# A decoder's block turn through DRAM: one VectorE transpose for 512 columns, 8 KB tiles, 2 KB stores, loads of two chunks, and later small loads at the start

## The chip, the cores and the metric

One core of a Trainium2 chip runs the whole kernel as one launch. The metric is the device time in microseconds of that launch. The kernel before took 2060.33 us, the median of three executions (2054.5 to 2066.38).

## The reference, cut to what matters

Two decoder layers act on x of shape (4, 512, 512) in float32. Each layer has three residual steps, and each step starts with a layer norm of x:

```python
x = x + attn0(layernorm(x))     # 16 query heads of 32, one key/value head        stage L0
x = x + xattn0(layernorm(x))    # mixes columns with a softmax made from ctx_1024  stage X0
x = x + ffn0(layernorm(x))      # 4-bit weights, 1408 inner, rms norm              stage FF
x = x + attn1(layernorm(x))     # 16 heads of 32                                   stage L1
x = x + xattn1(layernorm(x))    # 16 heads of 128, 8 key/value heads, ctx_1024     stage X1
x = x + ffn1(layernorm(x))      # 32 experts of rank 16, top 2                     stage R1
```

Stage X1 is the longest. For each of 4 batches and 16 heads it computes softmax(q k^T / sqrt(128)) as a 512 x 512 matrix and multiplies it by v. The softmax is made with tokens on the partitions. The product with v needs it turned, with keys on the partitions.

## The kernel before, in words

A batch's 512 tokens are QT = 4 tiles of 128 tokens, and its 512 columns are KC = 4 chunks of 128. x stays in SBUF as 16 tiles of 128 x 512 float32. To keep float32 accuracy on TensorE, an operand is split into a high and a low part (`split_sbuf`, L704: a cast to fp32r, on ScalarE or VectorE, and then a subtraction, on GpSimd or VectorE). `three` (L649) makes three matmuls for every product: high by high, high by low, low by high.

**Order of the work.** The kernel does not issue its instructions as it is written. `put` and `after` (L615, L621) place pieces of work on a time axis. Run in that order, they are recorded as tasks, and `arrange` (L327) plays a list scheduler on them with a cost for each instruction: each engine takes the ready task of the highest priority, and a tile is given a slot when a slot of its pool is free. Priorities come from a pass backwards from the end. 16 rounds are played, and the shortest plan gives the order on each engine and the slot of each tile. The times in `put` fix only the first round's order; no task waits for its `put` time. All tasks are then issued at L1845, the only line that the profile shows for them. Each engine works its queue strictly in order, SyncE's DMA queue (SP) too.

**Pools.** Per partition there are TBUFS = 50 tiles "t" of 2 KB (activations, high and low parts, the `ws` and `pt` landing tiles) and WBUFS = 17 tiles "w" of 4 KB (split weights, attention stacks, FF weights, and `tr`).

**The block turn** (`block_turn`, L756) turns four tiles of 128 tokens x 512 columns into four chunks of 128 columns x 512 tokens. It is used 79 times: for the 64 heads of X1 (tiles `pe`) and for 15 of the layer norms in FF, L1, X1 and R1 (tiles `h`). It has three steps:

- `turn(t)`: VectorE transposes tile t in blocks of 32 x 32, as two instructions of 256 columns into two `tr` tiles of the "w" pool, 8 instructions a turn.
- `away(j)`: for each half j, four stores on SP write `tr` to a DRAM scratch `turn`, 128 KB each, in pieces of 512 bytes. That is 8 stores a turn.
- `back(k)`: for each chunk k, one load on SP brings 256 KB, 2 KB a partition, into a "t" tile `pt`. Then `split_sbuf` makes `turnedh` and `turnedl`, which TensorE reads. That is 4 loads a turn.

In X1 a head's scores, `turn`, `away`, `back` and product with v (`weigh`) are placed about one period PER_X1 = 11.7 us apart in the plan (L1650 to L1657).

**The start.** x of batch 0 is loaded by SP (L573). `cols`, `mask8` and `scales16` are loaded on ScalarE's queue (L576 to L580). VectorE then makes `desc`, `scales` and `maskf` (L599 to L604) ahead of the first layer norm. `scales` is used from FF on, `maskf` from X1 on, `desc` in R1. The x of batches 1 to 3 are loaded by three 1 MB transfers, placed at -11, -10 and -9 us (L1034).

Of the kernel before, what the change touches and what calls it, by code (L numbers as in the profile page):

```python
# [10 lines left out]
F32 = mybir.dt.float32  # L11
# [22 lines left out]
NI = FI // P  # L34
# [3 lines left out]
LN_EPS = 1e-5  # L38
RMS_EPS = 1e-6
BIG = 1e30  # L40
TBUFS = 50
WBUFS = 17
START = 45.0
DQ = 50.0
PER_L0, PER_X0, PER_F1, PER_L1, PER_X1, PER_R1 = 16.5, 12.5, 6.1, 22.5, 11.7, 25.0
# [16 lines left out]
WARM = 24  # L62
LOOK = {"tensor": 99999, "vector": 99999, "scalar": 99999, "gpsimd": 99999, "sync": 99999}
T_X0, PER_A0 = 5.0, 15.0
NA = {"L0": 4, "X0": 4, "FF": 0, "L1": 0, "X1": 0, "R1": 0}
EARLY = "v1", "qk1", "o1"
ACT_JIT = True
EVAC = "AA01"
DT = 6
# [9 lines left out]
TINY = 2.0**-14  # L79
# [469 lines left out]
def decoder_kernel(ctx: ExitStack, tc: tile.TileContext, a: dict, out: bass.AP):  # L549
# [8 lines left out]
    nc = Recorder()  # L558
    PSUM = bass.MemoryType.PSUM

    def pool(name, bufs, n=None, **k):
        return Pool_(ctx.enter_context(tc.tile_pool(name=name, bufs=bufs or 1, **k)), bufs, n or name)

    base = pool("base", None)
    small = pool("small", 4)
    wp = pool("weights", WBUFS)
    tp_ = pool("tiles", TBUFS)
    dram = pool("scratch", None, space=bass.MemoryType.DRAM)
    ps = pool("ps", 1, space=PSUM)

# [4 lines left out]
    cols = base.tile([P, 19], F32, name="cols")  # L575
    nc.scalar.dma_start(cols, a["cols"])  # L576
    mask8 = base.tile([P, NB * QT], U8, name="mask8")
    nc.scalar.dma_start(mask8, a["mask_col"])
    scales16 = base.tile([P, 2 * NI * KC + NI * NT], F16, name="scales16")
    nc.scalar.dma_start(scales16, a["gu_cols"])  # L580
    scales = base.tile([P, 2 * NI * KC + NI * NT], F32, name="scales")
    ident = base.tile([P, P], F32, name="ident")
    make_identity(real, ident.real())
# [12 lines left out]
    desc_i = base.tile([P, NS], I32, name="desc_i")  # L596
    nc.gpsimd.iota(desc_i, pattern=[[-1, NS]], base=NS, channel_multiplier=0)
    desc = base.tile([P, NS], F32, name="desc")
    nc.vector.tensor_copy(desc, desc_i)  # L599
    n = 2 * NI * KC  # L600
    nc.vector.tensor_scalar(scales[:, 0:n], scales16[:, 0:n], 1.0 / TINY, None, ALU.mult)
    nc.vector.tensor_copy(scales[:, n:], scales16[:, n:])
    maskf = base.tile([P, NB * QT], F32, name="maskf")
    nc.vector.tensor_copy(maskf, mask8)  # L604


    warm = ps.pool.tile([P, S], F32, name="warm", tag="mm.0", bufs=1)
# [48 lines left out]
    def at(pr, *ix):  # L656
        return pr[0][ix], pr[1][ix]
# [72 lines left out]
    def weight(t, key, src, cols=None, keep=False):  # L730


        got = {}

        def load():
            if key in stored:
                got["w"] = wp.tile(stored[key].tile.shape, F32R, tag="w", name="w")
                nc.sync.dma_start(f32(got["w"]), f32(stored[key]))
            else:
                got["w"] = split_weight(key, src, cols, keep, act=ACT_JIT and keep)  # L740

# [14 lines left out]
    def block_turn(tiles, got):  # L756


        tr, dr = [None] * 2, [None] * 2

        def turn(t):
            for j in range(2):
                if t == 0:
                    tr[j] = wp.tile([P, 2 * S], F32, tag="w", name="tr")
                nc.vector.transpose(
                    tr[j].rearrange("p (b t i) -> p b t i", t=QT, i=HD)[:, :, t, :],
                    tiles[t][:, j * 2 * P : (j + 1) * 2 * P].rearrange("p (b i) -> p b i", i=HD),
                )

        def away(j):  # L770
            dr[j] = dram.tile([2, P, HG, P], F32, tag="turn", name="turn", bufs=DT)
            for n in range(HG):
                nc.sync.dma_start(
                    dr[j][:, :, n, :].rearrange("c (q j) n -> j (c q) n", j=HD),
                    tr[j][n * HD : (n + 1) * HD, :].rearrange("j (b n) -> j b n", n=P),
                    run=4 * P,
                )

        def back(k):
            pt = T(name="pt")  # L780
            nc.sync.dma_start(pt, dr[k // 2][k % 2].rearrange("p a n -> p (a n)"))
            got[k] = pair(name="turned")
            split_sbuf(
                [g.rearrange("p (t a i) -> p a t i", t=QT, a=HG) for g in got[k]],
                pt.rearrange("p (a t i) -> p a t i", t=QT, a=HG),
                3.5,
                True,
            )

        return (  # L790
            [lambda t=t: turn(t) for t in range(QT)],
            [lambda j=j: away(j) for j in range(2)],
            [lambda k=k: back(k) for k in range(KC)],
        )

# [112 lines left out]
    def group(t0, per, u, keys, values, done, on_dve, lead):  # L908
# [122 lines left out]
        e = t0 + per + SUMS  # L1031
        put(e, e, [sums])

    for b in range(1, NB):  # L1034
        put(
            -12 + b,
            -12 + b,
            [
                lambda b=b: nc.sync.dma_start(
                    x[:, b * QT : (b + 1) * QT, :], a["x"][b].rearrange("(t p) d -> p t d", p=P)  # L1040
                )
            ],
        )
# [56 lines left out]
    for b in range(NB):  # L1100
        tb = now + 4 * b * per - (A0 + 0.25) * per
        hT = layernorm_T(tb - (0.25 + LN0) * per, tb - 0.25 * per, b, NA["L0"], pool=b < SL)
        kv = {}
# [24 lines left out]
        for c in range(KC):  # L1128
            t0 = now + (4 * b + c) * per
            u = {}  # L1130

            def queries(pq, u=u, c=c):
# [7 lines left out]
                lambda k, c=c: wq0[k](slice(c * P, (c + 1) * P)),  # L1140
# [106 lines left out]
    for b in range(NB):  # L1247
# [148 lines left out]
    for i in range(NI):  # L1396
        t = DQ + (ff0 + NI * per - 45 - DQ) * i / NI
# [12 lines left out]
    for b in range(NB):  # L1410
        tb = now + 4 * b * per - (A1 + 0.2) * per
        hT = layernorm_T(tb - LN1 * per, tb, b, NA["L1"], b in DV["L1"])

# [20 lines left out]
        for k in range(QT):  # L1434
# [5 lines left out]
                lambda c, k=k, hT=hT, wv=wv: (at(hT[c], ALL, tok(k)), wv[c]()),  # L1440
                lambda pv, k=k, f=values: f(pv, k),
            )
        oT = []
        for c in range(KC):
            t0 = now + (4 * b + c) * per
            u = {}
            for j in range(2):
                n0 = j * D + c * P
                w = weight(
                    t0 - (A1 + 0.5 - 0.2 * j) * per,  # L1450
                    ("qk1", j, c),
                    chunks(a["wqkv1"][:, n0 : n0 + P]),
                    KC,
                    keep=True,
                )

                def turned(pq, j=j, c=c, u=u):
# [13 lines left out]
                    lambda k, w=w: w(slice(k * P, (k + 1) * P)),  # L1471
# [5 lines left out]
            def normalise(w, pd, c=c, oT=oT):  # L1477
# [18 lines left out]
                lambda h, k, v=v, c=c: v[k][:, (4 * c + h) * HD : (4 * c + h + 1) * HD],  # L1496
# [10 lines left out]
        for t in range(QT):  # L1507
# [5 lines left out]
                lambda c, t=t, oT=oT, wo=wo: (at(oT[c], ALL, tok(t)), wo[c]()),  # L1513
                lambda po, t=t, b=b: add_to_x(b * QT + t, po),
# [6 lines left out]
    for b in range(NB):  # L1521
        tb = now + NH * b * per
        cT = context(tb - 3.2 * per, b)
        hT = layernorm_T(tb - 1.9 * per, tb - 1.1 * per, b, NA["X1"], b in DV["X1"])
        mk = {}
# [8 lines left out]
        for g in range(4):  # L1534
# [21 lines left out]
            for j in range(2):  # L1556
# [28 lines left out]
            for i in range(4):  # L1585
# [9 lines left out]
                u = {"pe": [None] * QT, "pT": [None] * QT}  # L1595

                def queries(pq, u=u):
# [6 lines left out]
                    lambda k, w=wq: w(slice(k * P, (k + 1) * P)),  # L1604
# [326 lines left out]
```

## Time and profile before

| what | value |
|---|---|
| three executions | 2054.5, 2060.33, 2066.38 us |
| the profiled execution's own time | 2058.85 us |
| its span, first to last instruction | 2057.1 us |
| DVE / ACT / POOL busy | 90% / 60% / 58% of the span |
| DMA, q1 (SP's queue) | 349472 packets, 465.50 MB, 72.7% of 16 engines |
| chain that ended last | PE 65%, DVE 12%, DMA 12% |

The profile is read by stage. L0 ends near 340 us, X0 near 405, FF near 720, L1 near 1150, X1 near 1950, and R1 runs to the end. The profile's waits name what ended an engine's idle time. A row of instruction groups gives the busy time, the mean nanoseconds of one, and the idle time before them. All work has the line L1845, so rows are told apart by tile names.

### The profile page before, as it was taken

To read this page: it belongs to the slowest core of one execution; us is meant where nothing else is said; L and a number is where in the kernel's file an instruction comes from. 1 tells how busy PE (TensorE), PEld (TensorE's weight loads), DVE (VectorE), ACT (ScalarE), POOL (GpSimd) and SP (SyncE) were. 2 spreads that over 40 slices of the span, in tenths; PEclk is the share of its full clock that TensorE was granted. 3 is DMA by queue.
4 is the path that set the end of the run, shared out by engine and by line. 5 is a ranking of instruction groups with operands and counts; after the bars stand their busy time and mean duration, and the time that the engine had idled before them with its cause. 6 is when DMAs were issued, how large, how long until landed. Compare 5 with 4: busy or idle time off the path is not lost.

```text
span 2057.1 us, 31942 instructions
## 1 busy us (share of the span) xinstructions
PE 1984.3 (96%) x9728; PEld 1476.8 (72%) x9728; DVE 1848.7 (90%) x3645; ACT 1239.2 (60%) x2461; POOL 1195.0 (58%) x930
## 2 busy tenths in 40 slices
PE   7999999999999999999999999999999999999999
PEld 6755554778877856565656777787888777887677
DVE  8999998999999889898899898999999889998883
ACT  5876767467757355454546767676666557555520
POOL 5688889378777466867577445454454244233610
PEclk9999999999999999999999999999999999999999
DMA  7554444656758777777764889999999899988911
GB/s 254 198 187 149 144 159 145 232 185 231 261 171 296 222 229 240 211 243 221 222 169 141 246 236 272 288 288 294 299 299 304 246 307 292 317 255 247 273 60 58
DMA packets 350075, 467.57 MB, mean 227 GB/s; under 512 B 28944, under 2 KB 211472, under 8 KB 349904
## 3 DMA queue, kind: packets, MB, share of 16 engines
q1 hardware_dynamic: 349472, 465.50, 72.7%
q8 instruction: 77, 1.26, 0.3%
q14 instruction: 94, 0.77, 0.1%
q10 hardware_dynamic: 432, 0.04, 0.0%
HBM read 291.36 MB, written 173.93 MB: 226 GB/s over the span
## 4 chain that ended last, share of the span: by engine, by line
PE 65%; DVE 12%; DMA 12%; ACT 5%; issue 2%; SPq 2%; POOL 1%; ACTq 0%; DVEq 0%; POOLq 0%
PE mm L1845 65%; DMA pt<-turn 6%; DVE pe L1845 2%; SPq L1845 2%; DVE tr L1845 2%; DMA stack<-stack 2%; DVE nm L1845 2%; DMA turn<-tr 2%; ACT pT L1845 1%; DMA stack<-ql 1%; DVE x L1845 1%; ACT turnedh L1845 1%; ACT pe L1845 1%; DVE ol L1845 1%; DVE ql L1845 1%
## 5 line engine op out<-in xcount | busy, mean ns | idle before, releaser
L1845 POOL TENSOR_TENSOR turnedl<-pt,turnedh 128x512 fp32r<-128x512 f32 x249 | 328.8, 1334 | 407.2 <-ACT turnedh L1845 181.7
L1845 PE MATMUL mm<-turnedh,w 128*128 128x512 f32 x1120 | 414.6, 398 | 7.8 <-ACT turnedh L1845 3.0
L1845 DVE TENSOR_REDUCE nm<-mm 128x1 f32<-128x512 f32 x512 | 323.3, 678 | 35.3 <-PE mm L1845 34.5
L1845 PE MATMUL mm<-stack 96*128 96x512 f32 (+1 forms) x1024 | 325.8, 422 | 25.6 <-DMA stack<-stack 17.7
L1845 ACT ACTIVATE pT<-mm 128x512 f32<-128x512 f32 x512 | 273.2, 609 | 78.9 <-PE mm L1845 70.4
L1845 POOL TENSOR_TENSOR acc<-acc,pT 128x512 f32<-128x512 f32 x200 | 271.0, 1378 | 31.5 <-DVE acc L1845 12.6
L1845 PEld LDWEIGHTS mm<-stack 96*128 96x128 f32 (+1 forms) x1024 | 186.1, 192 | 140.5 <-issue 35.4
L1845 PE MATMUL mm<-turnedl,w 128*128 128x512 f32 x736 | 282.8, 394 | 1.2 <-POOL turnedl L1845 1.2
L1845 PEld LDWEIGHTS mm<-turnedh,w 128*128 128x128 f32 x1120 | 211.2, 189 | 65.7 <-ACT gu L1845 7.8
L1845 ACT ACTIVATE pe<-pe,nmc 128x512 f32<-128x512 f32 x256 | 184.6, 722 | 112.6 <-DVE nmc L1845 105.9
L1845 ACT CAST turnedh<-pt 128x512 fp32r<-128x512 f32 x291 | 176.5, 617 | 113.5 <-DMA pt<-turn 105.7
L1845 PE MATMUL mm<-w,oh 128*128 128x512 f32 x640 | 203.9, 391 | 5.6 <-ACT oh L1845 5.6
L1845 POOL TENSOR_TENSOR acc<-pT 128x512 f32<-128x512 f32 x118 | 155.6, 1333 | 77.2 <-ACT pT L1845 60.9
L1845 DVE STREAM_TRANSPOSE tr<-pe 128x256 f32<-128x256 f32 x512 | 198.3, 419 | 2.2 <-ACT pe L1845 2.0
L1845 DVE CUSTOM_DVE_ANT_0 pe<-mm,mb 128x512 f32<-128x512 f32 x256 | 169.7, 670 | 4.9 <-PE mm L1845 4.3
L1845 POOL TENSOR_TENSOR w<-ws,w 128x512 fp32r<-128x512 f32 x93 | 126.0, 1364 | 70.1 <-ACT w L1845 41.2
L1845 PEld LDWEIGHTS mm<-turnedl,w 128*128 128x128 f32 x736 | 139.1, 189 | 26.5 <-POOL turnedl L1845 2.7
L1845 ACT ACTIVATE gu<-mm,scales 128x512 f32<-128x512 f32 x173 | 113.5, 691 | 57.5 <-PE mm L1845 56.8
L1845 PEld LDWEIGHTS mm<-w,oh 128*128 128x128 f32 x640 | 118.9, 188 | 32.1 <-ACT oh L1845 8.0
L1845 POOL TENSOR_TENSOR gu<-gu 128x512 f32<-128x512 f32 x83 | 109.7, 1333 | 44.4 <-DVE gu L1845 33.0
L1845 DVE SCALAR_TENSOR_TENSOR gu<-mm,scales,gu 128x512 f32<-128x512 f32 x176 | 122.1, 738 | 2.4 <-PE mm L1845 2.3
L1845 PE MATMUL mm<-w,ol 128*128 128x512 f32 x320 | 123.7, 391 | 0.0
(235 smaller groups left out, 4543.9 us busy)
## 6 DMA issues: line engine op xcount, KB each, us to landing
turn<-tr SPq DMA_DIRECT2D x632, 128.0 KB
pt<-turn SPq DMA_DIRECT2D x316, 256.0 KB
w<-scr SPq DMA_DIRECT2D x148, 512.0 KB
stack<-stack SPq DMA_DIRECT2D x96, 384.0 KB
scr<-w SPq DMA_DIRECT2D x56, 512.0 KB
stack<-qh SPq DMA_DIRECT2D x96, 256.0 KB
w<-gu SPq DMA_DIRECT2D x44, 512.0 KB
w<-dn SPq DMA_DIRECT2D x44, 384.0 KB
```

Of the source, the lines that this page charges most:

```text
L1845: got = getattr(getattr(real, t.engine), name)(*[made(v) for v in a_], **{n: made(v) for n, v in k.items()})
```

## The change

The transpose of a tile becomes one instruction of 512 columns into one 8 KB tile `tr` of a new pool "big" with 2 slots. Four stores of 256 KB in 2 KB pieces replace eight of 128 KB in 512-byte pieces. Two loads of 512 KB in 1 KB pieces, into a 4 KB "w" tile `pt` that holds two chunks, replace four of 256 KB in 2 KB pieces. The pool "t" goes from 50 to 44 tiles and "w" from 17 to 16. `mask8` and `scales16` are loaded on SP and placed at 40 us, their four VectorE casts 4 us later; the x of batches 1, 2 and 3 are placed at -5, 50 and 110 us.

```diff
-TBUFS = 50
-WBUFS = 17
+TBUFS = 44
+WBUFS = 16
+BBUFS = 2
...
+T_X = -5.0, 50.0, 110.0
+T_TABLES = 40.0
...
-    nc.scalar.dma_start(mask8, a["mask_col"])
...
-    nc.scalar.dma_start(scales16, a["gu_cols"])
...
-    nc.vector.tensor_copy(desc, desc_i)
-    n = 2 * NI * KC
-    nc.vector.tensor_scalar(scales[:, 0:n], scales16[:, 0:n], 1.0 / TINY, None, ALU.mult)
-    nc.vector.tensor_copy(scales[:, n:], scales16[:, n:])
...
-    nc.vector.tensor_copy(maskf, mask8)
...
         def turn(t):
-            for j in range(2):
-                if t == 0:
-                    tr[j] = wp.tile([P, 2 * S], F32, tag="w", name="tr")
-                nc.vector.transpose(
-                    tr[j].rearrange("p (b t i) -> p b t i", t=QT, i=HD)[:, :, t, :],
-                    tiles[t][:, j * 2 * P : (j + 1) * 2 * P].rearrange("p (b i) -> p b i", i=HD),
+            if t == 0:
+                u["tr"] = big.tile([P, KC * S], F32, tag="b", name="tr")
+
+            nc.vector.transpose(
+                u["tr"].rearrange("p (e c t i) -> p c e t i", e=HG, c=KC, t=QT)[:, :, :, t, :],
+                tiles[t].rearrange("p (c e i) -> p c e i", c=KC, e=HG),
+            )
+
+        def away(n):
+            if n == 0:
+                u["dr"] = dram.tile([P, HG, KC * P], F32, tag="turn", name="turn", bufs=DT)
+            nc.sync.dma_start(
+                u["dr"][:, n, :].rearrange("(e j) s -> j e s", j=HD),
+                u["tr"][n * HD : (n + 1) * HD, :].rearrange("j (e s) -> j e s", e=HG),
+                run=4 * S,
+            )
+
+        def back(k):
+            if k % 2 == 0:
+                u["pt"] = wp.tile([P, HG, 2 * P], F32, tag="w", name="pt")
+                nc.sync.dma_start(
+                    u["pt"], u["dr"][:, :, k * P : (k + 2) * P], run=8 * P
                 )
-
-        def away(j):
-            dr[j] = dram.tile([2, P, HG, P], F32, tag="turn", name="turn", bufs=DT)
-            for n in range(HG):
-                nc.sync.dma_start(
-                    dr[j][:, :, n, :].rearrange("c (q j) n -> j (c q) n", j=HD),
-                    tr[j][n * HD : (n + 1) * HD, :].rearrange("j (b n) -> j b n", n=P),
-                    run=4 * P,
-                )
-
-        def back(k):
-            pt = T(name="pt")
-            nc.sync.dma_start(pt, dr[k // 2][k % 2].rearrange("p a n -> p (a n)"))
...
+    def tables():
+
+        nc.sync.dma_start(mask8, a["mask_col"])
+        nc.sync.dma_start(scales16, a["gu_cols"])
+
+        def cast():
+            n = 2 * NI * KC
+            nc.vector.tensor_copy(desc, desc_i)
+            nc.vector.tensor_scalar(scales[:, 0:n], scales16[:, 0:n], 1.0 / TINY, None, ALU.mult)
+            nc.vector.tensor_copy(scales[:, n:], scales16[:, n:])
+            nc.vector.tensor_copy(maskf, mask8)
+
+        after(4, cast)
+
+    put(T_TABLES, T_TABLES, [tables])
     for b in range(1, NB):
         put(
-            -12 + b,
-            -12 + b,
+            T_X[b - 1],
+            T_X[b - 1],
```

More of the change, by code (lines that the diff above doesn't have):

```diff
@@ L567, in decoder_kernel @@
     tp_ = pool("tiles", TBUFS)
+    big = pool("big", BBUFS)
     dram = pool("scratch", None, space=bass.MemoryType.DRAM)
@@ L756, in block_turn @@
     def block_turn(tiles, got):
-        tr, dr = [None] * 2, [None] * 2
+        u = {}
         def turn(t):
-            for j in range(2):
-                if t == 0:
-                    tr[j] = wp.tile([P, 2 * S], F32, tag="w", name="tr")
-                nc.vector.transpose(
-                    tr[j].rearrange("p (b t i) -> p b t i", t=QT, i=HD)[:, :, t, :],
-                    tiles[t][:, j * 2 * P : (j + 1) * 2 * P].rearrange("p (b i) -> p b i", i=HD),
-                )
-        def away(j):
-            dr[j] = dram.tile([2, P, HG, P], F32, tag="turn", name="turn", bufs=DT)
-            for n in range(HG):
-                nc.sync.dma_start(
-                    dr[j][:, :, n, :].rearrange("c (q j) n -> j (c q) n", j=HD),
-                    tr[j][n * HD : (n + 1) * HD, :].rearrange("j (b n) -> j b n", n=P),
-                    run=4 * P,
-                )
-        def back(k):
-            pt = T(name="pt")
-            nc.sync.dma_start(pt, dr[k // 2][k % 2].rearrange("p a n -> p (a n)"))
+            if t == 0:
[17 more added lines that the diff above has]
+                    u["pt"], u["dr"][:, :, k * P : (k + 2) * P], run=8 * P
+                )
             got[k] = pair(name="turned")
@@ L784, in back @@
                 [g.rearrange("p (t a i) -> p a t i", t=QT, a=HG) for g in got[k]],
-                pt.rearrange("p (a t i) -> p a t i", t=QT, a=HG),
+                u["pt"][:, :, k % 2 * P : (k % 2 + 1) * P].rearrange("p a (t i) -> p a t i", t=QT),
                 3.5,
@@ L791, in block_turn @@
             [lambda t=t: turn(t) for t in range(QT)],
-            [lambda j=j: away(j) for j in range(2)],
+            [lambda n=n: away(n) for n in range(HG)],
             [lambda k=k: back(k) for k in range(KC)],
```

## The prediction

> **What bounds the kernel now.** I read the engine totals first, then busy time by stretch of 100 us, then the waits inside the longest stage, X1, where 64 of the 79 turns are.
>
> ```profile
> span 2057.1 us, 31942 instructions
> ...
> PE 1984.3 (96%) x9728; PEld 1476.8 (72%) x9728; DVE 1848.7 (90%) x3645; ACT 1239.2 (60%) x2461; POOL 1195.0 (58%) x930
> ```
> ```profile
> 1000.00:1100.00 100.00, 93.82 (x470) 56.74 (x470) 89.75 (x125) 53.01 (x104) 71.52 (x54) 0.97 0.56 168
> 1300.00:1400.00 100.00, 98.97 (x447) 79.75 (x446) 95.19 (x236) 69.17 (x147) 55.48 (x42) 1.00 0.99 300
> 1500.00:1600.00 100.00, 97.72 (x450) 80.68 (x450) 91.36 (x232) 64.91 (x140) 46.88 (x36) 1.00 0.98 301
> 1900.00:2000.00 100.00, 94.90 (x436) 70.38 (x434) 84.54 (x217) 40.51 (x78) 45.20 (x35) 1.00 0.60 176
> ```
>
> The columns are the stretch, its length, then busy time of PE, PEld, DVE, ACT and POOL, the granted clock, the DMA share and GB/s. In X1 three resources are near full at once: PE 98 to 99%, DVE 91 to 95%, the DMA engines 98 to 99%. PE is the one that sets the end. Matmuls of 512 columns start 227 ns apart in the trace (the median of starts), and a head needs 54 of them: 12 for q, 12 for the scores, 12 for the product with v, and per head 6 for keys and values (24 for a group of 4 heads, the values counted at half width) and 12 for the output. That is 12.26 us a head and 785 us for 64, and X1 lasts about 800 us (1150 to 1950). So whatever relieves DVE and the DMA engines can win some 15 us here, and 20 to 25 with the tail of the stage, unless PE's own work shrinks, and that stays as it is.
>
> What opens PE's gaps in X1 (the waits of PE and of its weight loads, 1150 to 1960 us; total, times, longest):
>
> ```profile
> PE mm L1845 <- ACT turnedh L1845: 8.6, 9, 1.6
> PE mm L1845 <- POOL turnedl L1845: 6.5, 13, 1.5
> ```
> ```profile
> PEld mm L1845 <- POOL turnedl L1845: 17.9, 37, 1.9
> PEld mm L1845 <- ACT turnedh L1845: 15.1, 15, 2.0
> ```
>
> The turned chunks are first in both lists. With VectorE's own share (1.2 and 3.4 us) the matmuls stood idle 16.3 us for them and the weight loads 36.4 us. So the change works on the cause of most of what PE loses here; there is just little to lose.
>
> **The turn on the DMA engines.** The DMA queues of X1's middle, 1200 to 1900 us:
>
> ```profile
> DMA packets 191376, 198.53 MB, mean 284 GB/s; under 512 B 13973, under 2 KB 141816, under 8 KB 191313
> ...
> q1 hardware_dynamic: 191313, 197.81, 93.1%
> ...
> pt<-turn SPq DMA_DIRECT2D x232, 256.0 KB
> turn<-tr SPq DMA_DIRECT2D x462, 128.0 KB
> ```
>
> The trace's packet records of this stretch, sorted by size, have means of 32.0 ns for 512 B (126307 packets), 46.4 ns for 1 KB (1536), 95.3 ns for 2 KB (34777). A turn now stores 2048 packets of 512 B and loads 512 of 2 KB: 65.5 + 48.8 = 114.3 us, over 16 engines 7.15 us. After, it stores 512 of 2 KB and loads 1024 of 1 KB: 48.8 + 47.5 = 96.3 us, 6.02 us. A turn saves 1.13 us. The stretch holds 58 turns, so 65 us of its 652, and the share falls from 93% to about 84%. The bytes are the same. Bounds: the 1 KB price comes from few packets; were it half the 2 KB mean (47.7) the saving is 1.05 us, and if 2 KB stores cost no less per byte than the 512 B ones (128 ns) there is none.
>
> A rule speaks against this part. The Trainium skill, "DMA: Bandwidth & Descriptors", section "Specifications", puts the smallest transfer for line rate at 512 B, so by it the stores are at full rate already and the larger pieces buy nothing. The packets above disagree: per KB, 64.0 ns at 512 B against 47.7 at 2 KB. By the rule the DMA term would be 0, by the packets 1.13 us a turn.
>
> **SP.** Issues of stores last 463 ns and of loads 424 ns (medians), and a 512 KB load of `w` 0.46 us too, so size does not set them. 12 issues a turn (5.4 us) become 6 (2.7 us). Behind SP's waiting store stand the weight loads and other turns' loads. SP waited 117.2 us for `tr` in X1; that stays, since the store still waits for the last transpose. New is that the first load waits for the whole 1 MB rather than for 0.5 MB, and brings 0.5 MB rather than 0.25: 0.75 MB at 284 GB/s is 2.8 us later for the first chunk, while the last chunk comes no later. That eats part of the relief, and I credit the relief with only part of the gaps for it.
>
> **The turn on VectorE.**
>
> ```profile
> L1845 DVE STREAM_TRANSPOSE tr<-pe 128x256 f32<-128x256 f32 x512 | 198.3, 419 | 2.2 <-ACT pe L1845 2.0
> ...
> L1845 DVE SCALAR_TENSOR_TENSOR vl<-mm,maskf,vh 128x256 fp32r<-128x256 f32 x64 | 29.4, 460 | 1.9 <-ACT vh L1845 1.9
> ```
>
> No 512-column transpose is in this trace. One bound is twice the present one, 0.84 us, a gain of nothing. The other is from the nearest pair of one operation in both widths: `vl` takes 460 ns for 256 columns and `ql` 740 for 512, 1.61 times, so 0.67 us, a gain of 0.16 us a pair. I take 0.70, nearer to the second, as it is the only row pair that shows one operation in both widths. 256 pairs in X1 make 36 us less on DVE of some 730 busy. Were a write pattern with 2 KB strides slower, the nearest dearer row is a 512-column operation at 1.09 us (`turnedl` on DVE): 0.25 us more a pair, 64 us in X1, and DVE would then stand at 100% of it. Nothing in the trace excludes this; I keep it for the range.
>
> **X1, summed.** Both reliefs make `turned` earlier, and where a turned tile comes in time PE goes on at 227 ns. Gaps to close are between 16.3 us (idle of the matmuls) and the 20 to 25 above. I take 12 us, two thirds to a half, as `oh` and `qh` (7 us of PE's waits) are next late and the first chunk is later: -12, bounds 0 and -22.
>
> **FF, L1 and R1: 15 turns.** PE's gaps at them are few; the same share gives -2, bounds 0 and -4.
>
> **The start.**
>
> ```profile
> 6.22 0.18 DVE L1845 CAST maskf<-mask 128x16 f32<-128x16 uint8 x1 [1.82 <-DMA mask<-in_mask_col]
> 6.30 0.18 DVE L1845 CAST desc<-desc_i 128x32 f32<-128x32 int32 x1
> 6.38 0.69 DVE L1845 BATCH_NORM_STATS2 s<-x 128x6 f32<-128x512 f32 x1
> ```
>
> The chain that ended last begins with this mask load (4.54 us). Without it the first norm waits for x: the packet records show its four tiles (128 packets each) all started by 5.6 us, the first by 3.2. So statistics can start near 4.4 instead of 6.38: -2 us. The two loads cost SP two issues of 0.45 us at a time when it has pauses, and the four casts (0.74 us) land in L0, where DVE idles 5 to 10%. The x loads gain nothing for certain: they need no tile of a pool and wait for nothing, so the planner still issues them when SP is free, and 2.7 us of packets (512 of 2 KB at 84 ns on 16 engines) may or may not go behind the first weights. Bounds 0 and -5; I take -2.
>
> **The pools.** `tr` leaves "w" and `pt` enters it, two of each a turn; `pt` leaves "t", which loses 6. In L0, FF and L1, with few turns, this is simply less room. What "w" is worth shows in SP's waits from 350 to 1150 us:
>
> ```profile
> SPq L1845 <- PE mm L1845: 191.0, 113, 17.5
> ```
>
> These loads wait for a tile that PE still reads. Most are prefetches: PE's matmuls themselves stood idle only 14.6 us in the same stretch for `stack` loads. One tile of 17 less brings them 6% later. I take +2, bounds 0 and +15.
>
> **Sum.** -12 - 2 - 2 + 2 = -14. The profiled execution took 2058.85 us (1.75 around its span) and would come to 2045; the median shown is 1.5 us higher, so 2046.
>
> **Rivals.**
>
> 1. *PE is full already.* `turned` comes earlier, but the planner fills the room with other work and the gaps move to `oh` and `qh`. For it: 785 of 800 us are PE's own. Then X1 gives 2 to 4 and the start 2: 2055. The same follows if the start does not do what it says.
> 2. *Two 8 KB tiles are too few.* A half tile is held today from its first transpose to the landing of its stores: 6 to 8 us of transposes, 1, 2 of issues, about 4 of landing, some 13 in all, by matching transposes and stores in the trace; the longest spread of transposes in X1 is 20 us for heads and 44 for a norm. Two tiles at a head each 12.3 us allow 24.6 us. It decides when a norm's turn keeps one tile: heads then share one, 13 to 19 us against 12.3, so 1 to 7 us late for two or three heads, at 7 norms (X1 and R1). At 5 us each that is +35, less 14 gained elsewhere: 2081. Against it: the planner knows the pool and can draw a norm's transposes together.
> 3. *Less room in "w" and "t"* slows L0, FF and L1 at its upper bound of 15, and more stack loads come late as at 1030 us, where PE is at 94%: about +12 net, 2072.
>
> **How the numbers follow.** A measurement of this kernel can tell about 0.5% from no change, so faster means below 2050, slower above 2071. Forecast (2046, own range 2030 to 2054, partly over the line): 0.48. Rival 1: 0.24. Rival 2: 0.16. Rival 3: 0.12. The forecast's own range reaches into the same with 0.04 of its 0.48, so: faster 0.44, same 0.28, slower 0.28. The range begins where all terms are at their best (-22, -4, -5 and 0, in sum -31 from the median: 2029) and ends with rival 2 at 2081.
>
> **What would show it.** Right: the DMA share of X1 near 84%, the transpose near 0.70 us, PE's waits for `turnedh` and `turnedl` halved, the first BATCH_NORM near 4.4 us. Wrong: the transpose above 0.84 us; SP or DVE waiting long for the store of an older `tr` (rival 2); more PE waits for `stack` in L1 (rival 3); PE's waits in X1 unchanged in sum under other names (rival 1).

## The result, and the profile after

The kernel after takes 2071.12 us (median of 12 runs, 2064.47 to 2077.01) against 2059.07 for the kernel before (12 runs, 2052.24 to 2066.38): a ratio of 1.0058, 95% interval 1.0044 to 1.0073. It is slower by 12 us. The forecast was 13 us faster. The time lies inside the range, on the other side of no change.

The head of the profile after (its profiled execution took 2065.73 us):

```profile
span 2064.0 us, 30966 instructions
...
PE 1985.1 (96%) x9728; PEld 1475.3 (71%) x9728; DVE 1845.5 (89%) x3348; ACT 1234.9 (60%) x2463; POOL 1161.1 (56%) x909
...
DMA packets 261586, 467.47 MB, mean 226 GB/s; under 512 B 21360, under 2 KB 122992, under 8 KB 261424
...
q1 hardware_dynamic: 261280, 465.50, 71.5%
```

A quarter of the packets is gone (349472 to 261280 on q1) and their time has hardly moved: 72.7% of the engines' span to 71.5%. VectorE has 297 instructions fewer and 3 us less work. Two rows of the groups tell why:

```profile
L1860 DVE STREAM_TRANSPOSE tr<-pe 128x512 f32<-128x512 f32 x256 | 178.2, 698 | 3.7 <-ACT pe L1860 2.7
...
L1860 DVE TENSOR_TENSOR turnedl<-pt,turnedh 128x512 fp32r<-128x512 f32 x95 | 120.0, 1265 | 21.0 <-ACT turnedh L1860 16.0
```

The transposes fell from 198 us of busy time (512 of 419 ns) to 178. One takes the 0.70 us that was forecast, but the gain is 20 us and not 36: before, one of them stood right behind another 216 times, and there it starts 357 ns after the first, not 419 (medians), so that two had cost less than twice one. And VectorE now makes 95 of the low parts instead of 67, at 1265 ns instead of 1085, which is 47 us more; GpSimd makes as many fewer (249 to 221). It is not the freed time that moved them: of the kernels of the experiments below, the eleven that load two chunks at once make 86 to 113 low parts on VectorE (e9 makes 99, with the old transposes), and the seven that load one chunk make 53 to 76.

Busy time by stretch of X1 (stretch, length, PE, PEld, DVE, ACT, POOL, clock, DMA share, GB/s):

```profile
1300.00:1400.00 100.00, 95.28 (x429) 76.52 (x429) 92.17 (x193) 64.79 (x138) 43.52 (x34) 1.00 0.90 274
1500.00:1600.00 100.00, 94.77 (x421) 76.79 (x420) 88.97 (x185) 61.93 (x131) 33.59 (x25) 0.98 0.90 282
```

Before, the same stretches had PE at 99.0 and 97.7 and the DMA engines at 0.99 and 0.98. All three are less full now: none of them has become fuller than it was, PE simply waits more. What its weight loads wait for in X1 (1150 to 1960 us):

```profile
PEld mm L1860 <- ACT turnedh L1860: 17.7, 19, 2.4
PEld mm L1860 <- POOL turnedl L1860: 15.8, 31, 1.2
PEld mm L1860 <- ACT qh L1860: 7.9, 8, 1.9
```

With VectorE's shares (3.9 and 3.3) the weight loads wait 40.7 us for the turned chunks; it was 36.4. The waits that the change was to halve are all there.

The start did what was forecast, and more:

```profile
3.40 0.69 DVE L1860 BATCH_NORM_STATS2 s<-x 128x6 f32<-128x512 f32 x1 [0.88 <-DMA x<-in_x]
...
6.53 0.69 DVE L1860 BATCH_NORM_STATS2 s<-x 128x6 f32<-128x512 f32 x1 [1.42 <-DMA x<-in_x]
```

The first norm starts at 3.40 us rather than 6.38; the third of the four waits 1.42 us for x.

**Where the time goes, by stage.** Every kernel here makes the same 9728 matmuls, in differing order. I give each shape its full-rate time, add them up in the order of the trace, and read when each kernel has done the same share. Against before, the kernel after is 4 us ahead at 5% of the work (111 us), 4.6 behind at 9% (208 us), 5 ahead at 54% (1136 us, the beginning of X1), and 6.7 behind at the end. So **the stretch from there to the end, X1 and the rest of R1, loses 11.6 us**, where 12 were to be won. I call this "X1's change" below, and the lag at 54% "the first part". Both come from one profiled execution for each kernel, so a few us of them mean nothing; the profiled execution of e1 below, for one, was 12 us longer than that kernel's median.

### The profile page after: what moved, and what is told of

Its sections match the earlier page's. It is cut to its first block, busy times and chain, and to the rows that moved or that the text cites. A ratio compares the mean times of both kernels' runs of the same rounds, so it can differ in the third digit from the quotient of the medians.

```text
span 2064.0 us, 30966 instructions
## 1 busy us (share of the span) xinstructions
PE 1985.1 (96%) x9728; PEld 1475.3 (71%) x9728; DVE 1845.5 (89%) x3348; ACT 1234.9 (60%) x2463; POOL 1161.1 (56%) x909
## 3 DMA queue, kind: packets, MB, share of 16 engines
q1 hardware_dynamic: 261280, 465.50, 71.5%
## 5 line engine op out<-in xcount | busy, mean ns | idle before, releaser
L1860 POOL TENSOR_TENSOR turnedl<-pt,turnedh 128x512 fp32r<-128x512 f32 x221 | 293.4, 1341 | 403.4 <-ACT turnedh L1860 211.5
L1860 POOL TENSOR_TENSOR acc<-acc,pT 128x512 f32<-128x512 f32 x207 | 276.4, 1360 | 31.4 <-DVE acc L1860 15.8
L1860 ACT CAST turnedh<-pt 128x512 fp32r<-128x512 f32 x272 | 157.6, 616 | 106.7 <-DMA pt<-turn 102.1
L1860 POOL TENSOR_TENSOR w<-ws,w 128x512 fp32r<-128x512 f32 x89 | 119.8, 1354 | 110.1 <-ACT w L1860 84.0
L1860 DVE STREAM_TRANSPOSE tr<-pe 128x512 f32<-128x512 f32 x256 | 178.2, 698 | 3.7 <-ACT pe L1860 2.7
L1860 ACT ACTIVATE gu<-mm,scales 128x512 f32<-128x512 f32 x175 | 114.8, 687 | 40.7 <-PE mm L1860 40.1
L1860 DVE TENSOR_TENSOR turnedl<-pt,turnedh 128x512 fp32r<-128x512 f32 x95 | 120.0, 1265 | 21.0 <-ACT turnedh L1860 16.0
L1860 PE MATMUL mm<-pT,v 128*32 128x512 f32 x1024 | 124.4, 602 | 0.3
```

The lines of the kernel that those rows point to most:

```text
L1860: got = getattr(getattr(real, t.engine), name)(*[made(v) for v in a_], **{n: made(v) for n, v in k.items()})
```

## The experiments

All ratios are to the kernel before on the same chip, 95% intervals in brackets. Every kernel computes the whole reference.

**First: the parts alone.** e1 is before with the new start; e2 before with the smaller pools; e3 the new turn and pools with the old start; e4 before with one constant of the order's first round changed, to see what another order of the same work is worth.

```diff
# e2
-TBUFS = 50
-WBUFS = 17
+TBUFS = 44
+WBUFS = 16
# e4
-... PER_R1 = 16.5, 12.5, 6.1, 22.5, 11.7, 25.0
+... PER_R1 = 16.5, 12.5, 6.1, 22.5, 11.7, 26.0
```

> The kernel before with the new start alone (tables on SP at 40, x of batches 1 to 3 at -5, 50, 110), old turn, old pools. Before is 2059 us, after 2071. Room theory (the tiles taken from the pools cost the time) and turn theory (the turn's loads of two chunks behind 1 MB of stores cost it): the start is a gain of about 4 us, as the traces of before and after stand 4 us apart after 70 us: 2055. Order theory (every edit reshuffles the planned order of the instructions, and 12 us are the spread of that): anywhere from 2050 to 2068.

> The kernel before with 44 tiles t and 16 tiles w in place of 50 and 17, old turn, old start. Room theory: most of the loss shows, 2070 or more (above after, since tr still needs its two w tiles and pt its t tiles here). Turn theory: at most 3 us over before, 2059 to 2062. Order theory: anywhere from 2050 to 2068.

> After with the old start: new turn with its pools (44, 16, 2). Room theory and turn theory alike: after without the 4 us of the start, 2075. Order theory: anywhere from 2060 to 2085.

> A control: the kernel before with PER_R1 26 in place of 25, which only changes the order in which the first round of the planner takes the last stage, and so the order of all engines; same work, same pools. Room theory and turn theory: within 4 us of before, 2055 to 2063. Order theory: 6 us or more away from 2059 on either side.

e1 1.0001 [0.9983, 1.0018]; e2 1.0114 [1.0092, 1.0137]; e3 1.0119 [1.0092, 1.0147]; e4 0.997 [0.9955, 0.9985]. The start alone is worth nothing at the end. **Six 2 KB tiles and one 4 KB tile less cost 23 us (2082.97 against 2059.76)** in a kernel that is otherwise before. The new turn added to that (e3) changes nothing. Another order alone moves the time by 0.3%, so at least that much is the grain of every comparison below.

**Which pool.** e5 takes six tiles from "t" only, e6 one from "w" only, e7 is e1 with both.

> The kernel before with 44 tiles t alone (w stays 17). Both pools together cost 23 us. Theory X1-room (t is what X1 lives on: pe, pt, turned, keys, values): at least 15 of the 23 are here, 2075 or more, and they are lost after 1150 us. Theory w-room (the attention stacks of L0 and L1 and the weights): at most 6 are here, 2060 to 2066. An order change alone gave -0.3%, so 6 us either way decide nothing.

> The kernel before with 16 tiles w alone (t stays 50). Theory X1-room: at most 8 us of the 23, 2060 to 2068. Theory w-room: 15 or more, 2075 or more, lost before 1150 us in L0, FF and L1.

> The cell that is missing between after and its parts: new start and small pools, but the old turn (256-column transposes into two w tiles, 512-byte stores, loads of one chunk). After is 2071, pools alone 2083, start alone 2057. Theory that the new turn gives back part of the room (pt leaves t, tr leaves w) and relieves DVE and the DMA engines: slower than after by 8 or more, 2079 or above. Theory that the new turn gains nothing and only the start is worth 12 on top of small pools: 2071 within 5 us.

e5 1.0148 [1.0131, 1.0165]; e6 1.0178 [1.0163, 1.0193]; e7 1.021 [1.0195, 1.0225]. Each shortage alone costs as much as both in e2 or more: they do not add up. They lose most of it in the first part (13 to 27 us behind there in e2, e5, e6 and e7, another 5 to 8 after), spread over small waits; no row of PE's waits carries it. A part of it is time at a low granted clock (last section), in the first part 13.7 us before, 17.1 in e2, 18.8 in e5, 29.0 in e6 and 25.6 in e7. Whether the low clock makes such a loss or follows from PE's gaps is not shown. One of 17 tiles in "w" (e6) costs 35 us. From e7 to the kernel after only the turn differs, 2.1% to 0.58%: with small pools the new turn wins back three quarters of what they cost.

**Parts of the turn with large pools.** e8 keeps the transposes of 256 columns and pools of 50 and 17, lays out each half for 1 KB stores, and loads two chunks at once in 4 KB pieces into a "w" tile. e9 keeps before's transposes, stores and layout, and only loads two chunks at once, in 2 KB pieces. e10 is e8 with before's loads of one chunk, in 512 B pieces. All three have the new start.

```diff
 # e8, away(j); back(k) loads dr[k // 2] whole, run=32 * P
-            dr[j] = dram.tile([2, P, HG, P], F32, tag="turn", name="turn", bufs=DT)
+            dr[j] = dram.tile([P, HG, 2 * P], F32, tag="turn", name="turn", bufs=DT)
             for n in range(HG):
                 nc.sync.dma_start(
-                    dr[j][:, :, n, :].rearrange("c (q j) n -> j (c q) n", j=HD),
-                    tr[j][n * HD : (n + 1) * HD, :].rearrange("j (b n) -> j b n", n=P),
-                    run=4 * P,
+                    dr[j][:, n, :].rearrange("(e j) s -> j e s", j=HD),
+                    tr[j][n * HD : (n + 1) * HD, :].rearrange("j (e s) -> j e s", e=HG),
+                    run=8 * P,
 # e9, back(k)
-            pt = T(name="pt")
-            nc.sync.dma_start(pt, dr[k // 2][k % 2].rearrange("p a n -> p (a n)"))
+            if k % 2 == 0:
+                u["pt"] = wp.tile([P, 2, S], F32, tag="w", name="pt")
+                nc.sync.dma_start(u["pt"], dr[k // 2].rearrange("c p a n -> p c (a n)"), run=4 * S)
```

> New start, old pools (50, 17) and no 8 KB tiles: two 256-column transposes as before, but each half is laid out so that its four stores write 1 KB pieces and one load of 512 KB brings two chunks in 4 KB pieces, into a w tile. It has the fewer, larger DMA pieces and the paired loads without the 16 KB that the 8 KB tiles take. Room theory: with the room back and the DMA engines relieved it is at or below start alone (2057), 2045 to 2057. Theory that loads of two chunks hurt (both halves' splits at once, loads waiting for their stores on SP): slower than start alone by 5 or more, 2062 or above.

> Start alone (ratio 1.000 to before) with one edit in the turn: one load of 512 KB brings the two chunks of a half, into a w tile; transposes, 512-byte stores and 2 KB pieces as before, pools 50 and 17. Pairing theory (two chunks that land together make the loads wait at the head of SP's queue and bunch the splits, so X1 loses some 20 us as in the kernel with halves): ratio 1.008 or more, SP's wait for the stores in X1 above 80 us. Piece theory (what hurts in the kernel with halves is its pieces: 1 KB stores and loads that take longer than their medians): 1.004 or less, SP's wait near 40 us as in start alone.

> The kernel with halves (ratio 1.017: 1 KB stores, one load of two chunks) with each chunk loaded alone again, 256 KB in 512-byte pieces, into a t tile. Pairing theory: back near start alone, 1.006 or less. Piece theory: 1.012 or more, since 512-byte loads are no cheaper than the 4 KB ones they replace.

e8 1.0172 [1.0148, 1.0195]; **e9 0.9917 [0.9894, 0.9939], faster than both kernels**; e10 1.0059 [1.0044, 1.0073]. My theory that pairing the loads hurts fell with e9: there it is what helps. None of the kernels with larger pieces so far (after, e8, e10) is faster than before.

**Is the result one unlucky order?** e11 is the kernel after with e4's constant. e12 is the kernel after with a planner that expects a load 1.2 us later after the store it waits for, so that its order lets SP issue other transfers meanwhile.

```diff
 # e12, against after
-    "sync": {"tensor": 0.1, "vector": 0.1, "scalar": 0.0, "gpsimd": 0.1},
+    "sync": {"tensor": 0.1, "vector": 0.1, "scalar": 0.0, "gpsimd": 0.1, "sync": 1.2},
```

> A control: after with PER_R1 26 in place of 25, same work and pools, another planned order. If after's 1.006 is the change's own level: 1.002 to 1.010. If after is a lucky or unlucky order of a change whose level lies elsewhere (turn with old start stood at 1.012): outside of that.

> After, with the planner told that a transfer that reads what another wrote is ready 1.2 us later than it assumes (SP's loads wait 116 us in X1 for the turn's stores, each about 1.4 us). Theory that this wait at the head of SP's queue is what X1 loses: the wait falls below 50 us and the time goes to 1.000 or below. Theory that the wait is idle time that SP has: the wait falls and the time stays at 1.003 or more.

e11 1.0045 [1.0027, 1.0064]: the level stands. e12 1.0142 [1.0122, 1.0163]: SP's waits for `turn<-tr` in X1 fell from 116 to 93 us, not below the 50 us that its theory asked for, and the kernel became slower. Nothing here says that SP's waiting time as such is the loss: e9 has 92 us of the same wait and is the fastest kernel so far.

**The turn taken apart at small pools.** With the new start and 44 and 16 tiles held fast, e13 has the paired load of e9; e14 has that and the 512-column transposes in two 8 KB tiles, still with eight 512 B stores and the old layout. From e14 to the kernel after only the layout and the pieces differ, and with them the number of stores and what each load waits for. e15 is e9 under e4's other order, e16 the paired load with the old start.

```diff
 # e14, turn(t), against e13
+            if t == 0:
+                u["tr"] = big.tile([P, KC * S], F32, tag="b", name="tr")
+            nc.vector.transpose(
+                u["tr"].rearrange("p (b t i) -> p b t i", t=QT, i=HD)[:, :, t, :],
+                tiles[t].rearrange("p (b i) -> p b i", i=HD),
+            )
```

> Before with the new start, pools of 44 and 16 and one load of two chunks into a 4 KB tile; transposes and stores as before. Without the paired load this was 1.021 times before. Pairing theory (fewer waits for SP's loads is what the new turn gives back): 1.007 to 1.013, about 2080 us or less. Room theory (4 KB tiles are what is short, and a pair holds one for two chunks): 1.020 or more, since 16 such tiles now hold the loads as well. Piece theory (the 2 KB stores and the shorter transpose give it back): 1.018 to 1.024, no change by the pairing.

> The kernel after with the old layout in DRAM: 512-column transposes in two 8 KB tiles, pools of 44 and 16, but stores of 512 B pieces and paired loads in 2 KB pieces. Piece theory (2 KB stores at 59 ns a KB are a little cheaper than 512 B ones at 64): 0.2 to 0.5% slower than the kernel after, so 1.008 to 1.011. Rival (the pieces cost nothing or harm, as the paired load in 2 KB pieces was the best kernel so far): 1.000 to 1.005. If the 8 KB tile and the 512-column transpose give the room back, this is at least 0.8% under e13; if they do nothing, it is equal to e13.

> e9 (new start, 50 and 17 buffers, paired load alone) with PER_R1 at 26 rather than 25, which shifts the order of the work and no cost. Level: 0.989 to 0.995 of before, as e9's 0.992. Luck of one order: 0.996 to 1.000, the level of the start alone.

> Before with the paired load alone, the start as before. If the 0.8% of e9 is the pairing's: 0.990 to 0.995. If it needs the new start: 0.997 to 1.002.

e13 0.9996 [0.9978, 1.0014]; e14 1.0051 [1.0028, 1.0074]; e15 0.9908 [0.9874, 0.9942]; e16 0.9998 [0.9972, 1.0025]. e15 confirms e9. The paired load takes e7's 2.1% back to nothing, far past what any theory gave it; the 8 KB tiles with their transposes cost 0.5% on top; layout and pieces then add nothing to the total. That last zero is two opposed halves. The kernel after comes to X1 30 us ahead of e14 (the first part: 5 ahead of before, against 26 behind) and loses 29 us to it in X1. X1's halves repeat from kernel to kernel:

| kernels | how the turn goes through DRAM | X1's change, us | first part, us |
|---|---|---|---|
| e4, e1, e2, e5, e6, e7, e10 | one chunk a load | -6.6, +2.5, +5.4, +5.7, +5.7, +7.7, +2.1 | -0.2, +7, +13, +16, +21, +27, +9 |
| e9, e13, e14, e15, e16 | two chunks a load, 512 B stores by half, old layout | -11.4, -14.5, -17.0, -10.6, -17.4 | -6, +13, +26, -7, +11 |
| after, e11, e3, e12 | two chunks a load, 2 KB stores of all chunks, new layout | +11.6, +7.4, +10.7, +9.7 | -5, -2, +16, +19 |
| e8 | two chunks a load, 1 KB stores by half, 4 KB load pieces | +17.7 | +6 |

These values hang on the weights and on the cut: with other weights for the small matmuls, and the cut anywhere from 1075 to 1200 us, single ones move by up to 10 us (e9 from -8 to -19), but the second row stays below zero and all later rows above. They also hold time at a low granted clock. With 1.7 us taken off for each such window of 3.4 us (an estimate from the clock's records), the rows are -8 to +4, -11 to -18, +2 to +10 and, for e8, +15. So the second row stands apart from the others, and the third overlaps with the first.

The second row is the gain that I forecast for X1, and in the traces it comes from the load of two chunks alone. The rows of the casts that wait for the loads agree with it (X1, 1150 to 1950 us; idle time before the casts after the second bar). Before, then e14, then the kernel after:

```profile
L1845 ACT CAST turnedh<-pt 128x512 fp32r<-128x512 f32 x247 | 149.6, 617 | 89.9 <-DMA pt<-turn 82.4 <-PE mm L1845 2.2 <-POOL turnedl L1845 2.2
...
L1845 DVE CAST turnedh<-pt 128x512 fp32r<-128x512 f32 x24 | 14.9, 622 | 12.1 <-DMA pt<-turn 12.1
```
```profile
L1857 ACT CAST turnedh<-pt 128x512 fp32r<-128x512 f32 x225 | 130.5, 617 | 59.5 <-DMA pt<-turn 56.9 <-PE mm L1857 0.7 <-DVE tr L1857 0.6
...
L1857 DVE CAST turnedh<-pt 128x512 fp32r<-128x512 f32 x44 | 22.4, 508 | 7.6 <-DMA pt<-turn 7.6
```
```profile
L1860 ACT CAST turnedh<-pt 128x512 fp32r<-128x512 f32 x221 | 128.2, 616 | 82.0 <-DMA pt<-turn 77.6 <-PE mm L1860 3.9
...
L1860 DVE CAST turnedh<-pt 128x512 fp32r<-128x512 f32 x40 | 21.8, 548 | 15.0 <-DMA pt<-turn 14.9
```

The casts wait 94.5 us for the loads before, 64.5 in e14 and 92.5 after (63 in e9, 53 in e13). This alone doesn't put the kernels in order, as the casts of the kernel before wait as long as those of the kernel after. What PE's weight loads wait for in X1 (1150 to 1960 us) comes closer. The first rows of that in e14:

```profile
PEld mm L1857 <- POOL turnedl L1857: 8.9, 13, 1.1
PEld mm L1857 <- ACT turnedh L1857: 7.9, 7, 2.1
```

For turned chunks the weight loads wait 36.4 us before, 18.3 in e14 (15 to 21 in the second row of the table) and 40.7 in the kernel after. For everything together they wait 53 us before (41 to 56 in the first row), 30 in e14 (30 to 38 in the second), 64 in the kernel after (52 to 64 in the third) and 62 in e8. So the halved wait that was forecast exists, in the second row.

And the busy time of the whole stretch, e14 and then after:

```profile
1150.00:1950.00 800.00, 786.51 (x3589) 643.88 (x3587) 739.16 (x1554) 523.91 (x1114) 343.98 (x260) 1.00 0.94 284
```
```profile
1150.00:1950.00 800.00, 768.52 (x3447) 616.63 (x3445) 721.20 (x1490) 504.12 (x1073) 318.05 (x241) 1.00 0.89 278
```

e14 has the DMA engines busier (94% against 89%) and PE busier by 18 us. Freed DMA time did not buy PE time here.

**The tie.** In the new layout each of the four stores holds a part of every chunk, so both loads wait for all four; by halves, the first load needs only its own half. I matched the k-th turn's transposes, store issues, load issues and casts in X1 by their order, and took means in us after the turn's last transpose:

| kernel | last store issued | loads issued | casts of the four chunks start | last low part done |
|---|---|---|---|---|
| before | 5.2 | 6.7, 7.4, 9.6, 10.5 | 11.5, 12.4, 14.8, 15.8 | 18.4 |
| e9 | 3.9 | 4.5, 7.7 | 10.1, 10.5, 13.7, 14.2 | 17.1 |
| e14 | 5.9 | 7.7, 9.9 | 13.4, 13.9, 16.2, 16.8 | 19.9 |
| after | 3.7 | 8.9, 9.7 | 14.1, 14.5, 16.2, 16.7 | 19.7 |
| e17 | 4.6 | 9.8, 10.5 | 15.5, 15.9, 17.1, 17.7 | 21.0 |
| e18 | 5.4 | 7.1, 9.0 | 12.6, 13.1, 15.4, 16.1 | 19.1 |

After has its stores out 1.5 us sooner than before, and then 5.2 us pass until the first load. e17 puts this tie on e14's old layout and pieces (four stores of 512 B pieces over all four chunks). e18 takes it off the kernel after (eight stores of 1 KB pieces, a DRAM tile for each half).

```diff
 # e17, against e14
-        def away(j):
-            dr[j] = dram.tile([2, P, HG, P], F32, tag="turn", name="turn", bufs=DT)
-            for n in range(HG):
-                nc.sync.dma_start(
-                    dr[j][:, :, n, :].rearrange("c (q j) n -> j (c q) n", j=HD),
-                    u["tr"][n * HD : (n + 1) * HD, j * 2 * S : (j + 1) * 2 * S].rearrange("j (b n) -> j b n", n=P),
+        def away(n):
+            if n == 0:
+                u["dr"] = dram.tile([KC, P, HG, P], F32, tag="turn", name="turn", bufs=DT)
+            nc.sync.dma_start(
+                u["dr"][:, :, n, :].rearrange("c (q j) n -> j (c q) n", j=HD),
+                u["tr"][n * HD : (n + 1) * HD, :].rearrange("j (b n) -> j b n", n=P),
 # e18, against after; the load of two chunks reads dr[k // 2]
-            nc.sync.dma_start(
-                u["dr"][:, n, :].rearrange("(e j) s -> j e s", j=HD),
-                u["tr"][n * HD : (n + 1) * HD, :].rearrange("j (e s) -> j e s", e=HG),
-                run=4 * S,
-            )
+            for n in range(HG):
+                nc.sync.dma_start(
+                    dr[j][:, n, 0 : 2 * P].rearrange("(e j) s -> j e s", j=HD),
+                    u["tr"][n * HD : (n + 1) * HD, :].rearrange("j (e s) -> j e s", e=HG)[
+                        :, :, j * 2 * P : (j + 1) * 2 * P
+                    ],
+                    run=8 * P,
+                )
```

> e14 with its eight stores of a turn made into four, each of all four chunks, still in 512 B pieces and the old layout; both loads of two chunks now wait for all four stores, as in the kernel after. If the tie is what loses: the first load is issued 8.5 to 10 us after the last transpose rather than 7.7, the stretch after 1150 us gives 0 to 15 us more than before rather than 17 less, and the whole is 1.010 to 1.020 times before. If the layout and its pieces lose: as e14, 1.002 to 1.008, with the gain of about 17 us in that stretch kept.

> The kernel after with its four stores of a turn made into eight, four for each two chunks in 1 KB pieces and into a DRAM tile of their own, so that the first load waits for four of them alone; loads in 1 KB pieces as in the kernel after; the price that the planner gives to a store is set to the bytes it really moves. If the tie is what loses: first load 1 to 3 us earlier, the stretch after 1150 us 10 us or more shorter than in the kernel after, the whole 0.992 to 1.002. If the layout and its pieces lose (e8, untied with 1 KB stores, lost 18 us in that stretch): as the kernel after or worse, 1.004 to 1.017.

e17 1.0133 [1.0106, 1.0161], first load at 9.8 us, X1's change +11.7 where e14 has -17.0. **The tie, with four stores in place of eight, costs 29 us in X1**, of which 7 are time at a low granted clock (e14 lost none there). In the whole it is 0.8%, 17 us, as e14 comes to X1 26 us late and e17 only 7. The two differ in more than the tie: a store takes 1.01 us to issue in e17 and 0.475 in e14 (medians), and packets of 512 B take 34.7 ns against 31.4 (1200 to 1900 us). How much of the loss these make is not separated. The casts of e17 and its stretch:

```profile
L1857 ACT CAST turnedh<-pt 128x512 fp32r<-128x512 f32 x231 | 133.0, 616 | 71.7 <-DMA pt<-turn 69.5 <-DVE tr L1857 1.2 <-PE mm L1857 0.3
...
L1857 DVE CAST turnedh<-pt 128x512 fp32r<-128x512 f32 x31 | 16.6, 539 | 17.5 <-DMA pt<-turn 14.9 <-PE mm L1857 2.3
```
```profile
1150.00:1950.00 800.00, 767.32 (x3464) 624.17 (x3463) 718.41 (x1491) 517.16 (x1104) 322.66 (x245) 0.99 0.94 277
```

The casts wait 84.4 us again, the weight loads 30.7 us for turned chunks and 56 in all, and PE is at 767 of 800, as in the kernel after, with the DMA engines as busy as in e14. But e18 is at 1.0074 [1.0052, 1.0096], with X1's change at +11.3: its first load comes 1.8 us earlier than in the kernel after, its casts wait 72.5 us, and X1 gains next to nothing (7 of its 11.3 us are time at a low granted clock, 2 of the kernel after's 11.6). Its weight loads still wait 35.8 us for turned chunks, although these are ready sooner after the transpose. So the tie, with what comes with it in e17, is enough to lose the gain, and its removal is not enough to get it: the new layout with its 1 KB pieces, or the order that is planned for it, loses it in another way too (e8, untied with 1 KB stores, says the same). Which way, I cannot show. It is not DMA time (89% in e18), and not the time from transpose to cast, which e8 has shortest of all (9.2 us). That both orders come from a planner that expects other durations is possible, and not shown.

## Why the prediction was wrong, point by point

- **X1, -12: wrong, +11.6. This is the step that failed, "both reliefs make `turned` earlier".** The gain was to follow from cheaper packets, with a part given up because the first load waits for the whole 1 MB. Of these two, the delay was sized rightly, and the relief on the DMA engines was 0.19 us a turn and not 1.13. The first load is issued 2.2 us later than before and its first cast starts 2.6 us later, against 2.8 worked out. The last cast, forecast no later, starts 0.9 later. So PE's weight loads wait 40.7 us for turned chunks where 36.4 were to be halved. I set the delay against 1.13 us a turn of DMA time as if both were small; in e17 waiting for all four stores, with what else differs from e14, costs some 29 us of X1. Why X1 stays slow in e18, without that wait, is open. The gain itself exists, at 11 to 17 us, in all five kernels that load two chunks in the old layout with stores by half. I had given the paired load no gain beyond its issues.
- **DMA, 7.15 to 6.02 us a turn: mis-sized.** The packet records of X1 (1200 to 1900 us) of the kernel after have 115.0 ns for 2 KB (34084) and 51.3 for 1 KB (59904). A turn then takes 32 x 115.0 + 64 x 51.3 ns = 6.96 us: 0.19 saved instead of 1.13, and the stretch's share is 89.4%, not 84. I priced 2 KB stores by before's 95.3 ns, whose packets were loads, and that price did not hold in the kernel after. Direction need not be all of it: e18 and e8 have 5376 packets of 2 KB each in this stretch, none of them a turn's, and these took 108.4 and 94.5 ns. The rule that was weighed against this, in the Trainium skill, "DMA: Bandwidth & Descriptors", section "Specifications" (line rate from 512 B on, so nothing to gain), came much closer than my packets did: per KB, 64.0 ns at 512 B before and 57.5 at 2 KB after.
- **Transpose, 0.70 us: right** (698 ns). Its 36 us on VectorE were 20, as pairs overlapped before, and the low parts on VectorE, more of them and longer, took 47 us more.
- **SP, 12 issues to 6: right in number, its worth not shown.** e9 saves two of the twelve and gains, the kernel after saves six and loses, and no run changes the issues alone. I had read from equal times that size does not set the time of an issue, and this did not hold: in the kernel after a store takes 0.50 us and a load 0.58 (medians), where before had 0.46 and 0.42, and in e17 a store takes 1.01.
- **The start, -2: right in place, gone at the end.** First norm at 3.40 us (forecast 4.4), 4 us ahead at 111 us, and e1 is at 1.0001. Yet with the paired load it decides: e9 0.9917 against e16 0.9998. The X1 changes of the two do not differ that way (-11 and -17); the first parts do (-6 and +11). Why an early lead survives in one and not in the other is not settled.
- **The pools, +2, bounds 0 and +15: mis-sized.** Alone they cost 23 us (e2), above the upper bound. I had counted late prefetches for one tile of 17; e6 has 35 us for that tile. In the kernel after itself the first part does not show this (-5); of the eleven other kernels with a pool of 44 or 16, nine stand there at +7 to +27 and two at -2 and +5, against -7 to +11 at 50 and 17. A part of that is the clock: in its first part the kernel after loses 8.5 us to a low granted clock, before 13.7 and those eleven 13.7 to 29.0. Why its clock falls less there is not shown.
- **Rivals.** The sign is that of rival 3 (2072; measured 2071). Its sum, not its mechanism, was met: pools cost more than it said, and PE waits less for stack loads between 340 and 1100 us than before (6.1 us for its largest row against 12.2). Rival 2: VectorE waited for the store of an older `tr` 0.9 us in all of X1; two 8 KB tiles cost 0.5% together with the transposes (e13 to e14), 11 us and not 35. Rival 1's sign, waits unchanged in sum, is there (40.7 us against 36.4), but under the same names.

## What to carry to other kernels

When transfers are merged, ask first which of them the reader of the data needs first: a store that carries a part of every chunk makes every load wait for all stores, and in e17, which has that and little else against e14, X1 lost more than any piece size gave. Price a packet by a row of the same direction as well as the same size, and expect it to differ from kernel to kernel. In a kernel whose order a planner makes from pools of tiles, a tile taken from a pool has to be tried by itself: one of 17 cost more than the whole change moved.

## What the runs showed of the hardware

- Packets of one size differ from kernel to kernel, and the direction is one thing that differs: in X1 2 KB took 95.3 ns before (loads of `pt` and weights) and 115.0 after (mostly stores), 1 KB 46.4 and 51.3, and 512 B 32.0 before (mostly stores) and 29.1 in e10 (mostly loads).
- VectorE's operations overlap by some 75 ns when they stand back to back: transposes of 256 columns last 419 ns and start 357 ns apart. Two small ones thus cost less than their durations add up to.
- One subtraction varies much on VectorE: `turnedl` of one shape took 1085 ns on average in the kernel before and 1265 after, where the middle 80% lie between 0.69 and 1.64 us; the 8 of 95 that run beside hardly any such operation of GpSimd took 0.68 us (median). The mean doesn't follow the number: 107 took 1185 ns in e15, and 86 took 1318 in e18.
- The granted clock falls to half in windows of 3.4 us, one or a few in a row, each worth 1.7 us at most. Their sum was 13.7 us before, 10.2 after, and 17.1 to 34.1 in the other kernels here (e11 least, e6 and e12 most); about a third of the windows lie between 850 and 1110 us. Some of the first part's spread is this. The Trainium skill, "TensorE: Matmul & The Clock Gate", section "Part 1: The HAM clock gate", gives a free-running window of about 3.4 us and half rate after an idle one, which agrees with the length and the depth here.
